# Other durations in the in-kernel list scheduler of a two-layer transformer block

## The chip, the cores and the metric

The kernel runs on one core of one Trainium2 chip. The metric is device time in microseconds (us) of one execution. TensorE (PE) multiplies, VectorE (DVE), ScalarE (ACT) and GpSimd (POOL) do the element work, and SyncE (SP) issues the DMAs. Each engine takes its instructions in the order in which they were written to it and waits on semaphores for what it reads, so a late input holds everything behind it on that engine.

## What is computed

Two layers on an input of 2 x 512 x 512, all in float32. `_layernorm`, attention and feed-forward are the usual ones:

```python
x = L0_attn_hidden_states                                        # (2, 512, 512)
x = x + _layernorm(_L0_attn_ref(_layernorm(x), Wq, Wk, Wv, Wo))  # 32 heads, 8 for K and V, rotary, causal
x = x + _layernorm(_L0_ffn_ref(_layernorm(x), A, B, W, bias))    # one linear map with a low-rank part
x = x + _layernorm(_L1_attn_ref(_layernorm(x), Wq, bq, ...))     # 32 heads, q and k normalised, not causal
x = x + _layernorm(_L1_ffn_ref(_layernorm(x), w1, w3, w2, ...))  # silu(h1) * h3, width 1376, low-rank parts
```

## The kernel before

**Tiling.** Tokens are tiles of 128 rows (four per batch), features are chunks of 128, and head size is 128. A product is made exact to float32 from halves: every operand is split into hi + lo in a faster 32-bit matmul format, and `mm3` (line 393) adds hi hi, hi lo and lo hi in PSUM. So each operand costs a copy (hi) and a subtraction (lo) on the other engines, and TensorE runs three matmuls in place of one.

**Work.** A unit is two heads of one batch: 32 units for layer 0, 32 for layer 1, then six feed-forward units for each batch. A unit has projections, scores with softmax, the product of P^T with V, and the output projection that is added to `y`. In most units ("lag") P^T is not made on TensorE: `softmax_tail` (line 681) transposes 32 x 32 blocks on VectorE, stores them to a DRAM buffer (`pc` in layer 0, `pd` in layer 1), reads them back with the blocks in place, and makes hi (a copy on ACT or DVE) and lo (a subtraction on POOL or DVE). In layer 1, q and k take a similar way (`flip`, line 1097, through `kdq` and `kdk`). Only then can `av_items` (line 839) issue the matmuls into `ps_oy` that use P^T.

**What sets the order.** The order of all instructions is computed while the program is built, by a list scheduler in the kernel's own code. It keeps a clock in us for each engine:

- `Engine.cost` (line 70) gives the duration of an ACT, DVE or POOL instruction from its engine, its operation, the number of columns and whether its source is PSUM.
- `Engine.__getattr__` (line 98) issues the instruction and advances the engine's clock. For a DMA it sets when the transfer is expected to have landed. For the others it keeps in `banks` when a PSUM bank is next usable, and in `last` when the result can be read.
- `mm`, `tp` and `pe` (lines 388, 401, 378) advance TensorE's clock.
- A piece of work is a generator. When it yields nothing, its next stage is put off until `last`, the time at which its newest result is expected (`step`, line 273).
- `streams` (line 345) walks a main list (scores, then P^T V) and streams of fills (`q` and `v` projections, `o` output projections, `a` the P^T V of lagged heads). It issues the next main item if what it reads is expected to be there and its tiles are free, and else a fill, from up to `ahead` places further on.
- `pick` (line 127) chooses, for a subtraction, addition, scaling or copy, the engine with the least expected end plus its duration times a weight; the weights and `ahead` differ by phase (`PHASES`). In the long phase of layer 1 they are 0.5 for DVE and 0.25 for POOL and ACT.

These clocks never enter the program. They only decide the order on each engine's queue and the choices of `pick`; semaphores do the waiting on the chip. PSUM has eight banks in the planner's list, and the large SBUF tiles are slots of one arena, named `ar` in the profile; all instructions stand at line 102, where `Engine.__getattr__` issues them.

Of the kernel before, what the change touches and what calls it, by code (L numbers as in the profile page):

```python
# [21 lines left out]
P = 128  # L22
# [7 lines left out]

LAT = 0.1
FIRST = "x0 x1 x2 k x3 q r v y o z"
# [24 lines left out]
class Item:  # L57
    """a piece of TensorE's work, to be issued when cond holds"""

# [4 lines left out]
class Engine:  # L64
    """An engine that keeps its order of issue, with a clock (us) of its work."""

# [3 lines left out]
    def cost(self, op, args, kw):  # L70
        out = args[0]
        n = 1
        for d in out.shape[1:]:
            n *= d
        src = args[1] if len(args) > 1 else out
        if op in ("bn_stats", "tensor_reduce"):
            n = max(n, nbytes(src) // (4 * src.shape[0]))
        psum = getattr(src, "space", None) == PSUM
        if self.name == "scalar":
            c = n / 1200 + (0.05 if psum else 0.093)  # L80
            for x in ("scale", "bias", "accum_out"):
                c += 0.093 if isinstance(kw.get(x), bass.AP) else 0
            return c
        if op in ("bn_stats", "bn_aggr"):
            return n / 960 + 0.2
        if self.name == "vector" and op == "tensor_scalar" and not psum:
            return n / 1326 + 0.07
        if self.name == "vector":
            return n / 960 + 0.07
        if op == "memset":  # L90
            return n / 960 + 0.07
        if len(args) > 3 and args[3] == ALU.pow:
            return 0.169 * n + 0.27
        if op == "tensor_tensor":
            return 0.00217 * n + 0.115
        return 0.00083 * n + 0.245

    def __getattr__(self, op):
        f = getattr(self.eng, op)

        def g(*args, **kw):
            r = self.k.tc.keep_in_program_order(f(*args, **kw))  # L102
            if self.name == "sync":
                k = self.k
                ram = args[0].space == bass.MemoryType.DRAM
                run = 4 * args[0].shape[-1]
                k.hw = max(k.hw + (0.62 if ram else 0.475), k.now + 0.6)
                k.dma = max(k.dma, k.hw + 0.6) + nbytes(args[0]) / 0.36e6 * (2 if run < 512 else 1)
                k.last = max(k.last, k.dma + 0.9)
            elif self.name in ("scalar", "vector", "gpsimd"):  # L110
                k = self.k
                t = max(self.free, k.now + LAT)
                banks = {x.name for x in args if isinstance(x, bass.AP) and x.space == PSUM}
                for x in banks:
                    t = max(t, k.banks.get(x, 0.0))
                self.free = t + self.cost(op, args, kw)
                for x in banks:
                    k.banks[x] = self.free + LAT
                k.last = max(k.last, self.free)
            return r  # L120
# [3 lines left out]
class Engines:  # L124
    WEIGHT = dict(vector=1.0, scalar=0.5, gpsimd=0.0)

    def pick(self, *cands):
        """issue the one of the candidates (engine, op, args...) that is done first"""
        def score(x):
# [20 lines left out]
    def mul(self, out, a, s):  # L150
        """by a factor of each row"""
        self.pick(("gpsimd", "tensor_scalar", out, a, s, 1.0, ALU.mult, ALU.mult),
# [3 lines left out]
    def copy(self, out, a):  # L156
        """from PSUM"""
        self.pick(("scalar", "copy", out, a), ("vector", "tensor_copy", out, a))
# [8 lines left out]
class Kern:  # L167
    """Work is written as items: functions, or generators that yield the time
    (of TensorE's work) after which their next stage is to be issued."""

# [30 lines left out]

# [1 line left out]
    def slot(self, tag):  # L203
# [12 lines left out]

    # the large tiles: a half or the whole of a slot each (halves of one type only in a slot)
    HALF = dict(W=2, Wk=1, nat=2, v=2, PT=2, TN=2, KT=2, raw=1, bb=1, bqk=1, qk=1, P=1, x=1, A=1, T=1, xn=1, pt=1, ot=1,
# [52 lines left out]

# [1 line left out]
    def step(self, g):  # L273
# [22 lines left out]
    def phase(self, i):  # L296
        """what is tuned for each phase of the work"""
        for k, v in PHASES[i].items():
# [26 lines left out]
    def wait(self, tag, n=1):  # L325
        """in a stage: until n slots are free, first come first served"""
        q = self.queues.setdefault(tag, [])
# [6 lines left out]
    def low(self, eng):  # L334
        """in a stage of low priority: until the engine has nothing issued to it"""
        e = getattr(self.nc, eng)
# [8 lines left out]
    def streams(self, main, fills, bg):  # L345
        """Issue the streams of items, each in its order: a fill when its nominal place in
        main has come, or main waits; bg starts at its nominal place."""
        mi = bi = idle = 0
# [27 lines left out]

# [1 line left out]
    def pe(self, t):  # L378
        """t: at the full clock, which TensorE has after a busy tick only"""
        s = max(self.clk, self.now)  # L380
# [7 lines left out]
    def mm(self, out, l, r, start, stop):  # L388
        self.nc.tensor.matmul(out, l, r, start=start, stop=stop)
        n = r.shape[-1]  # L390
        self.pe(n / 2400 + 0.0026 if r.dtype == F32R else n / 600 + 0.005)

    def mm3(self, out, pairs, start=True, stop=True):
        """exact hi/lo products: hi hi + hi lo + lo hi"""
        n = len(pairs)
# [5 lines left out]
    def tp(self, out, in_):  # L401
        self.nc.tensor.transpose(out, in_, self.ident)
        self.pe(0.109)

# [1 line left out]
    def setup(self):  # L406
# [33 lines left out]

# [1 line left out]
    def split(self, hi, lo, raw):  # L442
        """hi + lo = raw exactly"""
        nc = self.nc
# [33 lines left out]

# [1 line left out]
    def ln_stats(self, src):  # L480
# [68 lines left out]
    def resid(self, b, tt, lvl):  # L549
        """x of level lvl + 1 = x + LN(y); returned short of a constant of each row"""  # L550
        nc = self.nc
# [42 lines left out]
    def boundary(self, b, tt, lvl):  # L594
        """from the finished y of level lvl on"""
        x = yield from self.resid(b, tt, lvl)
# [18 lines left out]

# [1 line left out]
    def out_proj(self, b, first, last, ot, w, badd, lvl):  # L617
        """y += O Wo over the heads of this unit"""
        def one(tt):
# [61 lines left out]
    def softmax_tail(self, st, j, qt, ps, bias, scale, w):  # L681
# [13 lines left out]
        if not st.get("lag"):  # L695
            st["p", j, qt] = pr
            return
        # P^T = 32 x 32 blocks transposed on VectorE, and the blocks put in place on their way through DRAM
        yield from self.wait("T")
# [60 lines left out]
    def unit_done(self, st):  # L760
        """after the last use of V"""
        if st["vlast"]:
# [4 lines left out]
    def pv_items(self, st, j, voff, causal, bias):  # L767
        """transposes of P, then O^T = V^T P^T, split"""
        box = {}
# [69 lines left out]
    def av_items(self, st, j, voff, bias):  # L839
        """O^T = V^T P^T by halves of the queries, split"""  # L840
        box = {}
# [41 lines left out]

# [1 line left out]
    def l0_init(self):  # L885
# [11 lines left out]
    def l0_zero(self):  # L897
        """the parts of pd0 that stay unused"""
        nc = self.nc
# [113 lines left out]

# [1 line left out]
    def l1_init(self):  # L1015
# [18 lines left out]
    def l1_pre(self, hp, b, w, lag):  # L1034
# [62 lines left out]
        def flip(n):  # L1097
            """the transposes as 32 x 32 blocks on VectorE, put in place on their way through DRAM"""
            nat = st["nat" + n]
# [92 lines left out]

# [1 line left out]
    def f0_init(self):  # L1194
# [38 lines left out]

# [1 line left out]
    def f1_init(self):  # L1235
        """rows 0:16, 32:48, 64:80 of the pieces: hi of a low-rank factor, lo in block k; others 0"""
        nc, a = self.nc, self.a
# [150 lines left out]
    def f1_post(self, js, b, sts, last):  # L1388
        """y += g W2 over the chunks of units js"""
        def one(tt):  # L1390
# [29 lines left out]

# [1 line left out]
    def run(self, nu0=16, nu1=16, nf=6):  # L1422
        # at the ends of a layer's units some run batch by batch, each then with weights of its own
        units = []
# [17 lines left out]
        def pre(n):  # L1442
            """early, mid items and state of unit n"""
            if n not in sts:
# [43 lines left out]
        for k in FIRST.split():  # L1488
            for f in todo[k]:
                self.do(f)  # L1490
        # weights start this many units before (early, mid, late parts)
        bgs = {}
# [143 lines left out]
def _layout(i):  # L1636
    """Layouts of the arrays only: transposes and tilings."""
    n = {k: np.asarray(v) for k, v in i.items()}
# [44 lines left out]
```

## Time and profile before

| | |
|---|---|
| time, median of 3 runs | 2113.08 us (2110.2 to 2115.16) |
| span of the profiled execution | 2117.8 us |
| mean granted TensorE clock | 0.993 |
| TensorE, VectorE, ScalarE, GpSimd busy | 97%, 85%, 63%, 68% of the span |
| TensorE matmuls; VectorE instructions | 12605; 4210 |
| DMA | 370.54 MB, 175 GB/s in the mean |

The profile comes from one execution, for which it gives the span from the first to the last instruction. The names are tiles of the program: `ps_pj` projections, `ps_s` scores, `ps_oy` P^T V and output products, `ps_tr` transposes, `ar` any large tile. In a list of groups, a line has engine, operation, output and inputs, shape and count, then the busy us in total and the mean ns of one, then the engine's idle time before these and what ended it. A list of waits has the waiting instruction, who ended the wait, the us in total, how many times, and the longest. A releaser is inferred from semaphores.

### The profile page before, as it was taken

Reading aid. Unit: us, or ns where it says so; the run is one execution under the profiler, and the core shown is the slowest. Engines: PE = TensorE matmul, PEld = TensorE weight load, DVE = VectorE, ACT = ScalarE, POOL = GpSimd, SP = SyncE. Lnnn points to the kernel's source line nnn. Section 1 sums busy time; section 2 is a strip of 40 time slices with the busy share of each in tenths; the row PEclk is TensorE's granted clock in tenths of the full one; section 3 lists DMA queues with packets and bytes.
Section 4 is the critical chain, followed back from the end, with each engine's and each line's share of the span. In section 5 each row is a group of like instructions: output and inputs, shape, how many; then the busy total and the mean of one; then the engine's idle time right before and its main releaser. Section 6 shows DMA issues by size and latency. Waiting matters only on the chain.

```text
span 2117.8 us, 41211 instructions
## 1 busy us (share of the span) xinstructions
PE 2056.7 (97%) x12605; PEld 1827.5 (86%) x12605; DVE 1801.4 (85%) x4210; ACT 1337.7 (63%) x3247; POOL 1446.3 (68%) x1786
## 2 busy tenths in 40 slices
PE   8999999999999999999999999999999999989998
PEld 7888888888888798889899999999999898977886
DVE  7998899899888889889889999899989988888534
ACT  5776677577766668776666666666667666664212
POOL 5686678688875567877677777777777776774212
PEclk9999999999999999999999999999999999999999
DMA  2476567577652235887877777777777787763021
GB/s 98 127 183 166 145 185 183 143 200 199 177 159 66 71 103 166 244 232 223 227 202 229 220 227 211 207 221 219 225 206 232 213 240 212 224 178 93 31 67 44
DMA packets 476566, 370.54 MB, mean 175 GB/s; under 512 B 117400, under 2 KB 424488, under 8 KB 476344
## 3 DMA queue, kind: packets, MB, share of 16 engines
q1 hardware_dynamic: 476344, 367.91, 60.9%
q8 instruction: 99, 1.62, 0.3%
q14 instruction: 123, 1.01, 0.2%
HBM read 232.12 MB, written 135.66 MB: 174 GB/s over the span
## 4 chain that ended last, share of the span: by engine, by line
PE 54%; DMA 12%; DVE 9%; SPq 3%; issue 2%; POOL 2%; ACT 2%; DVEq 0%; ACTq 0%; POOLq 0%
PE ps_pj L102 23%; PE ps_oy L102 19%; PE ps_s L102 10%; DVE ar L102 6%; SPq L102 3%; DMA pd<-ar 3%; DMA ar<-pd 2%; POOL ar L102 2%; DMA kdk<-ar 2%; ACT ar L102 2%; DMA ar<-kdq 2%; DMA kdq<-ar 2%; PE ps_tr L102 1%; DMA ar<-pc 1%; DVE m L102 1%
## 5 line engine op out<-in xcount | busy, mean ns | idle before, releaser
L102 POOL TENSOR_TENSOR ar<-ar,ar 128x256 fp32r<-128x256 f32 (+4 forms) x1223 | 1058.3, 887 | 456.6 <-ACT ar L102 333.6
L102 PE MATMUL ps_oy<-ar,ar 128*128 128x256 f32 (+2 forms) x4014 | 832.2, 342 | 28.7 <-DVE ar L102 14.0
L102 PEld LDWEIGHTS ps_oy<-ar,ar 128*128 128x128 f32 x4014 | 653.5, 190 | 133.1 <-DVE ar L102 22.5
L102 ACT CAST ar<-ar 128x256 fp32r<-128x256 f32 (+3 forms) x1166 | 531.5, 490 | 305.4 <-DMA ar<-pd 117.1
L102 PE MATMUL ps_pj<-ar,xh 128*128 128x256 f32 (+1 forms) x3392 | 635.2, 285 | 0.9 <-POOL ar L102 0.6
L102 PEld LDWEIGHTS ps_pj<-ar,xh 128*128 128x128 f32 x3392 | 536.0, 190 | 14.5 <-POOL ar L102 1.1
L102 PE MATMUL ps_pj<-ar,xl 128*128 128x256 f32 (+1 forms) x1696 | 482.9, 285 | 0.0
L102 DVE STREAM_TRANSPOSE ar<-ar 128x256 f32<-128x256 f32 (+3 forms) x688 | 347.9, 533 | 16.9 <-DMA pd<-ar 9.7
L102 DVE TENSOR_TENSOR ar<-ps_pj,ar 128x512 f32<-128x512 f32 (+2 forms) x448 | 305.4, 683 | 52.5 <-PE ps_pj L102 44.8
L102 PE MATMUL ps_s<-ar,ar 128*128 128x512 f32 (+2 forms) x1252 | 338.5, 376 | 8.6 <-DVE ar L102 4.7
L102 PEld LDWEIGHTS ps_pj<-ar,xl 128*128 128x128 f32 x1696 | 322.9, 190 | 2.1 <-DVE xl L102 0.7
L102 PE MATMUL ps_pj<-xh,ar 128*128 128x512 f32 x816 | 286.6, 399 | 0.7 <-ACT xh L102 0.7
L102 DVE TENSOR_TENSOR y<-ps_oy,y 128x512 f32<-128x512 f32 x272 | 184.8, 680 | 81.8 <-PE ps_oy L102 80.2
L102 PEld LDWEIGHTS ps_s<-ar,ar 128*128 128x128 f32 x1252 | 214.5, 189 | 44.0 <-DVE ar L102 12.6
L102 DVE TENSOR_TENSOR ar<-ar,ar 128x256 fp32r<-128x256 f32 (+5 forms) x328 | 207.9, 652 | 51.1 <-ACT ar L102 50.1
L102 ACT ACTIVATE ar<-ps_s,mr,rq 128x512 f32<-128x512 f32 x256 | 198.6, 777 | 46.7 <-DVE mr L102 36.9
L102 PEld LDWEIGHTS ps_pj<-xh,ar 128*128 128x128 f32 x816 | 154.0, 189 | 31.7 <-ACT xh L102 1.1
L102 DVE TENSOR_REDUCE m<-ps_s 128x1 f32<-128x512 f32 x256 | 170.9, 673 | 6.2 <-PE ps_s L102 5.0
L102 ACT ACTIVATE ar<-ar,ri 128x512 f32<-128x512 f32 (+3 forms) x245 | 149.6, 621 | 38.3 <-DVE ri L102 37.1
L102 POOL TENSOR_SCALAR ar<-ar,ri 128x512 f32<-128x512 f32 (+3 forms) x202 | 133.0, 661 | 54.3 <-DVE ri L102 48.9
L102 PE MATMUL ps_pj<-xl,ar 128*128 128x512 f32 (+1 forms) x408 | 161.2, 395 | 0.0
L102 ACT ACTIVATE ar<-ps_s,m 128x512 f32<-128x512 f32 (+3 forms) x256 | 133.8, 526 | 23.4 <-DVE m L102 14.8
(91 smaller groups left out, 2105.5 us busy)
## 6 DMA issues: line engine op xcount, KB each, us to landing
pd<-ar SPq DMA_DIRECT2D x240, 256.0 KB, 3.7
ar<-pd SPq DMA_DIRECT2D x480, 128.0 KB, 3.3
ar<-pc SPq DMA_DIRECT2D x200, 128.0 KB, 3.0
ar<-in_wq SPq DMA_DIRECT2D x86, 256.0 KB, 4.1
ar<-in_wo SPq DMA_DIRECT2D x86, 256.0 KB, 3.6
kdk<-ar SPq DMA_DIRECT2D x31, 512.0 KB, 4.8
ar<-kdk SPq DMA_DIRECT2D x124, 128.0 KB, 4.0
kdq<-ar SPq DMA_DIRECT2D x31, 512.0 KB, 5.1
```

Of the source, the lines that this page charges most:

```text
L102: r = self.k.tc.keep_in_program_order(f(*args, **kw))
```

## The change

Only the scheduler's figures change; `PHASES` and all loops stay. Matmuls become longer (`COL` us per column and 0.006 each, at least 0.109). A matmul now also marks its PSUM bank as readable only `PTAIL + LAT` after its end. The time between two dependent instructions, a flat 0.1, becomes 0.06 plus a `TAIL` of the engine that wrote. The landing of a DMA is expected 1.0 us later. Several DVE, ACT and POOL durations change: DVE instructions with an SBUF source get longer, an accumulated sum on ACT costs 0.2, the power function on POOL gets a larger fixed part. Comments and documentation strings that the diff also removes are left out here.

```diff
-LAT = 0.1
+LAT = 0.06
+TAIL = dict(scalar=0.1, vector=0.078, gpsimd=0.04)
+PTAIL = 0.175
+LAND = 1.9
+COL = 0.0004395
...
         if self.name == "scalar":
-            c = n / 1200 + (0.05 if psum else 0.093)
-            for x in ("scale", "bias", "accum_out"):
-                c += 0.093 if isinstance(kw.get(x), bass.AP) else 0
+            c = n / 1200 + (0.06 if psum else 0.095) + (0.2 if "accum_out" in kw else 0)
+            for x in ("scale", "bias"):
+                c += 0.095 if isinstance(kw.get(x), bass.AP) else 0
             return c
         if op in ("bn_stats", "bn_aggr"):
-            return n / 960 + 0.2
+            return n / 960 + 0.15
         if self.name == "vector" and op == "tensor_scalar" and not psum:
-            return n / 1326 + 0.07
+            return max(n / 870, 0.07)
         if self.name == "vector":
-            return n / 960 + 0.07
+            return n / 960 + (0.07 if psum else 0.12 if n > 8 else 0.07)
         if op == "memset":
             return n / 960 + 0.07
         if len(args) > 3 and args[3] == ALU.pow:
-            return 0.169 * n + 0.27
+            return 0.16 * n + 0.4
         if op == "tensor_tensor":
-            return 0.00217 * n + 0.115
+            return 0.00217 * n + 0.14
         return 0.00083 * n + 0.245
...
-                k.last = max(k.last, k.dma + 0.9)
+                k.last = max(k.last, k.dma + LAND)
...
                 self.free = t + self.cost(op, args, kw)
+                done = self.free + TAIL[self.name]
                 for x in banks:
-                    k.banks[x] = self.free + LAT
-                k.last = max(k.last, self.free)
+                    k.banks[x] = done + LAT
+                k.last = max(k.last, done)
...
     def mm(self, out, l, r, start, stop):
         self.nc.tensor.matmul(out, l, r, start=start, stop=stop)
         n = r.shape[-1]
-        self.pe(n / 2400 + 0.0026 if r.dtype == F32R else n / 600 + 0.005)
+        self.pe(max(n * COL + 0.006, 0.109) if r.dtype == F32R else 4 * n * COL)
+        self.banks[out.name] = self.clk + PTAIL + LAT
...
     def tp(self, out, in_):
         self.nc.tensor.transpose(out, in_, self.ident)
         self.pe(0.109)
+        self.banks[out.name] = self.clk + PTAIL + LAT
```

## The prediction

> **What bounds the kernel now.** First the page's shares of busy time, then the slices: matmul runs nearly everywhere, VectorE (DVE) is next.
>
> ```profile
> PE 2056.7 (97%) x12605; PEld 1827.5 (86%) x12605; DVE 1801.4 (85%) x4210; ACT 1337.7 (63%) x3247; POOL 1446.3 (68%) x1786
> ```
>
> A busy share of 97% does not tell how much of it is waiting, because a matmul counts as busy from its start to its drained end. So next the timeline of TensorE in a dense stretch, where the start of one matmul to the start of the next is its real price.
>
> ```profile
> 1605.21 0.40 PE L102 MATMUL ps_pj<-ar,xh 128*128 128x256 f32 x2
> 1605.45 0.28 PE L102 MATMUL ps_pj<-ar,xl 128*128 128x256 f32 x1
> 1605.57 0.40 PE L102 MATMUL ps_pj<-ar,xh 128*128 128x256 f32 x2
> 1605.81 0.28 PE L102 MATMUL ps_pj<-ar,xl 128*128 128x256 f32 x1
> ```
>
> Three matmuls of 256 columns take 0.36 us, 0.12 each, though each shows 0.28 busy. Over the whole trace the median step from start to start is 119 ns (256 columns, 7156 of them), 231 (512, 4445), 175 (384, 384), 109 (348 transposes, and each of 256 records of the full-precision products). The sum, with 3.4 us for eight large full-precision records, is 851.6 + 1026.8 + 67.2 + 37.9 + 27.9 + 3.4 = 2014.8 us. The first matmul starts at 7.3 us, the last at 2107.8: 2100.5 us of stream, so 85.7 us of steps longer than their median, and 17.3 us at the two ends. That is all the order of issue can touch: 4% of the span.
>
> Where it is lost shows in the count of matmuls per stretch of 53 us (columns: stretch, its length, then busy us and count of PE, PEld, DVE, ACT, POOL, granted clock, DMA share, GB/s).
>
> ```profile
> 848.00:901.00 53.00, 50.57 (x347) 45.83 (x347) 47.38 (x106) 39.07 (x91) 43.85 (x53) 1.00 0.86 247
> 901.00:954.00 53.00, 49.25 (x318) 44.33 (x318) 44.44 (x93) 39.41 (x88) 41.15 (x50) 0.97 0.80 232
> 1590.00:1643.00 53.00, 53.00 (x384) 49.93 (x383) 49.13 (x114) 35.78 (x82) 39.27 (x46) 1.00 0.79 232
> 1749.00:1802.00 53.00, 49.48 (x316) 45.12 (x315) 42.92 (x95) 33.48 (x78) 35.30 (x41) 0.94 0.75 205
> 1855.00:1908.00 53.00, 45.09 (x240) 37.19 (x239) 47.33 (x104) 36.20 (x74) 37.59 (x52) 0.94 0.59 165
> ```
>
> With the same mix of work, 384 matmuls fit where nothing waits, and only 318 and 316 in the lead-in and the end of layer 1's attention. By steps, the 85 us fall so: 5.8 us to 53; 8.3 in 53 to 583; 10.8 in 583 to 795 (change of layer); 22.9 in 795 to 1060 (lead-in of layer 1); 9.2 in 1060 to 1696; 12.4 in 1696 to 1855; 14.1 in 1855 to 1908 (change to the last feed-forward); 1.5 after. The granted clock of 0.94 is a consequence of the stops, inside the sum.
>
> Last the waits: whom TensorE waits for, then who stops the queues behind it (engine and what it issues, who ended the wait; us in total, times, longest).
>
> ```profile
> PE ps_oy L102 <- DVE ar L102: 14.0, 17, 2.2
> PE ps_tr L102 <- ACT ar L102: 11.4, 7, 7.3
> PE ps_oy L102 <- POOL ar L102: 8.5, 14, 1.5
> ```
> ```profile
> ACT ar L102 <- PE ps_pj L102: 161.0, 87, 8.8
> ACT ar L102 <- DMA ar<-pd: 117.1, 62, 4.2
> ACT ar L102 <- PE ps_oy L102: 70.2, 76, 5.2
> ```
> ```profile
> SPq L102 <- DMA pd<-ar: 212.8, 105, 4.7
> ```
>
> TensorE waits for halves of P^T that DVE or POOL has not finished; upstream ScalarE (ACT), in order, sits on landings and PSUM groups that have not come, with later work behind it, and SP's queue holds its next DMAs behind stores not yet landed.
>
> **The change part by part.** No instruction is added or removed by a duration. What moves is the order on each queue, and through `pick` which engine takes a subtraction, copy or scaling.
>
> *Matmuls.* The old plan charges 7156 x 0.1093 + 4445 x 0.2159 + 384 x 0.1626 + 37.9 + 128 x 0.2183 + 3.4 = 1873 us (two records are one full-precision product). The new charges 0.1185, 0.2310, 0.1748 and 0.225: 2012 us, the trace's 2015. The old plan's TensorE thus ran 7% ahead. One rule speaks against the change: the Trainium skill's page "TensorE: Matmul & The Clock Gate", section "Back-to-back issue gap", gives an isolated step as columns / 2.4 + 2.5 ns, 215.8 and 109.2 ns, just the old charges; it adds that weight loads move the spacing in a real stream. By the rule the new charge is 7% too high and 1873 us of work would leave 227 us of stalls; by the row (119 and 231 ns, with next to no waits in 1590 to 1643) there are 86. I take the row.
>
> *Landings (LAND 0.9 to 1.9).* From the planner's formula a 128 KB read from `pd` lands 0.475 + 0.6 + 0.36 + 0.9 = 2.34 us after its issue begins, now 3.34; a 256 KB store 2.85, now 3.85.
>
> ```profile
> pd<-ar SPq DMA_DIRECT2D x240, 256.0 KB, 3.7
> ar<-pd SPq DMA_DIRECT2D x480, 128.0 KB, 3.3
> ```
>
> The rows say 3.7 and 3.3: the new figure is right to 0.2. Each P^T goes through both, so the old plan is 2.0 us early there.
>
> *Visibility (LAT, TAIL, PTAIL).* One hop was 0.1; it becomes 0.16 behind ACT, 0.138 behind DVE, 0.10 behind POOL and 0.235 behind a matmul. A PSUM addition of 512 was 0.603 and stays so, plus the 0.078 tail = 0.681; its row has 680 ns.
>
> *Vector instructions.* A 512 exponential with its sum was 0.756, now 0.877. A 256 subtraction on DVE goes from 0.337 to 0.387, on POOL from 0.670 to 0.696.
>
> ```profile
> L102 DVE TENSOR_TENSOR ar<-ar,ar 128x256 fp32r<-128x256 f32 x223 | 134.3, 621 | 23.5 <-ACT ar L102 23.0
> L102 POOL TENSOR_TENSOR ar<-ar,ar 128x256 fp32r<-128x256 f32 x853 | 641.5, 769 | 300.8 <-ACT ar L102 236.3 <-DVE ar L102 36.7 <-DVE r L102 11.3
> ```
>
> With tail and LAT the DVE subtraction is now expected after 0.525 (before 0.437), against 0.621 busy: still early, by less. In the long phase of layer 1 the weights are 1.5 on DVE and 1.25 on POOL and ACT: a subtraction's scores move 44 ns towards POOL, a copy 75 ns towards ACT, a 512 scaling from DVE 0.684 against ACT 0.766 to 0.883 against 0.771. So scalings leave DVE: 53 of 320 are there, 53 x 0.669 = 35 us at most over the kernel, spread on ACT (63% busy) and POOL (68%). Of the 223 subtractions perhaps 30 move, 30 x 0.77 = 23 us of POOL. Both are hidden: POOL is busy 39 to 44 of 53 us in the rows above. Without that cover each late subtraction would be a wait of TensorE of 0.15 us (0.769 less 0.621), 4.5 us.
>
> *What it is worth.* A P^T chain is expected 2.0 (landings) + 0.12 (exponential) + 0.14 (scores visible) + about 0.25 (subtraction, hops) = 2.5 us later than before. Most of the stops are single steps under 2.4 us, within the plan's error, so an order made with the right figures can put other matmuls there. Lower bound of the effect in 795 to 1060 and 1696 to 1855: nothing; upper bound: all 35.3. I take half, 17.6, since there is other work (projections) but PSUM has only eight banks. In the two changes of layer (24.9) the chain is layernorm, transposes and weights, with no detour through DRAM: I take a fifth, 5. Ends (17.3): unchanged, since nothing else exists to be put there. Places that ran well and are reordered by chance: 8 lost, bounded by 0 and by the slower rival. Net 17.6 + 5 - 8 = 14.6, so 2117.8 - 15 = 2103 us of span. The page gives the profiled execution by its span alone; that stands 4.7 us above the runs' median of 2113.1, and I carry this over: 2098.
>
> Nobody is made to wait by a new semaphore. What is late next, where a stop goes, is DVE: 47 to 49 of 53 us busy.
>
> **The rivals.** *A, the repair above*, 2098. For it: ACT idles 117 us on `pd` landings and 231 on matmul groups, SP 213 on stores, all waits that a late expectation reorders. Against it: in 1060 to 1696 the same errors of the plan cost only 9 us. Own range: 2078 (all 35 us regained) to 2108 (5 regained).
>
> *B, nothing to gain.* The chains are really too long for the lead-in, and the steady stages keep their slack: 2109 to 2117, I say 2113. For it: nearly no stall in 636 us of layer 1 despite a 7% error.
>
> *C, fills overtake the chain; slower.* With P^T expected 2.5 us later, the stream lets projections and output products go first (up to `ahead`, 15 to 45 places). Their PSUM additions, 0.68 us each, enter DVE's queue ahead of the transpose or subtraction that P^T needs, and DVE has only 4 to 6 us free in 53. Place: layer 1's attention from 795 to 1855, 30 of its units of two heads. It decides where the additional DVE work before a subtraction exceeds the chain's slack. At one more late addition for each of 60 heads it is 60 x 0.68 = 41 us, less A's 15: 2113 + 26 = 2139; with two, 2180. For it: the steady part, 1060 to 1696, can only lose. Against it: matmuls charged 7% more give DVE more room in the plan, and scalings leave it.
>
> **How the numbers follow.** A 0.52, B 0.10, C 0.38. The time is A's, 2098. About 0.2%, 4 us, is what the measurement can tell from no change: faster takes 0.50 (A without its upper edge), same 0.12, slower 0.38. The range starts at A's low end less a little, 2080, and reaches into C past its first price to 2150; 1 in 10 lies above (two late additions), under 1 in 10 below. A's own range is 2078 to 2108.
>
> **What would show it.** Right: over 345 matmuls in the stretches at 901 and 1749; ACT's wait for `pd` well under 117 us and SP's for `pd` stores under 213; ACT's waits for `ps_pj` and `ps_oy` under 231; fewer DVE scalings than 53; the same medians of 119 and 231 ns. Wrong: more long steps in 1060 to 1696 than 9 us, with `ps_oy` waiting for DVE, which is C; or those waits of ACT and SP gone while TensorE's long steps stay near 85 us, which is B: then they were never on its path. A new stop at a change of layer above 14 us would also break the forecast.

## The result, and the profile after

The change is a little slower: 2118.8 us in the median of 9 runs (2117.5 to 2131.0) against 2111.5 of before in the same comparison (2104.2 to 2115.3), a ratio of 1.0055, interval 1.0035 to 1.0076. The forecast was 2098, faster. The range held the time; the direction was wrong.

First a warning that the two profiles give. The span after is 2115.8 us, which is less than the 2117.8 of the profile before. The execution profiled after took 2117.64 us as a run, so a run is its span plus 1.8 us. By that the execution profiled before took 2119.6 us, longer than any of its timed runs: it was an unusually long one. A second profile of the same kernel (e1 below) has a span of 2109.0. It is the one to compare with.

The page's shares, of the profile after:

```profile
PE 2049.8 (97%) x12605; PEld 1824.6 (86%) x12605; DVE 1762.6 (83%) x4125; ACT 1358.4 (64%) x3285; POOL 1477.3 (70%) x1831
```

There are as many matmuls as before; VectorE has 85 instructions fewer, POOL 45 and ACT 38 more. `pick` has moved work, as the new durations make it. The median steps from start to start of a matmul are again 119, 231, 175 and 109 ns, so it is once more only the long steps that differ.

The counts of matmuls per stretch of 53 us, after (stretch, length, busy us and count of PE, PEld, DVE, ACT, POOL, clock, DMA share, GB/s):

```profile
689.00:742.00 53.00, 46.11 (x260) 37.92 (x259) 45.83 (x123) 33.63 (x79) 28.86 (x46) 1.00 0.24 80
901.00:954.00 53.00, 49.38 (x344) 45.30 (x343) 47.73 (x98) 40.22 (x95) 42.67 (x47) 1.00 0.89 257
1590.00:1643.00 53.00, 52.49 (x383) 49.47 (x382) 45.97 (x106) 34.90 (x80) 41.23 (x51) 1.00 0.80 231
1749.00:1802.00 53.00, 50.00 (x341) 45.43 (x340) 45.89 (x96) 37.02 (x83) 43.43 (x51) 1.00 0.84 226
1855.00:1908.00 53.00, 44.64 (x235) 36.48 (x234) 47.63 (x103) 34.25 (x69) 31.68 (x46) 0.94 0.51 149
```

and of before in its second profile:

```profile
689.00:742.00 53.00, 50.42 (x293) 42.03 (x293) 44.86 (x116) 32.05 (x74) 25.96 (x48) 1.00 0.22 75
901.00:954.00 53.00, 50.34 (x331) 45.73 (x330) 44.65 (x94) 38.28 (x86) 41.48 (x49) 0.97 0.79 236
1749.00:1802.00 53.00, 49.20 (x322) 45.12 (x321) 42.12 (x97) 33.53 (x78) 36.04 (x46) 0.94 0.81 223
```

The end of layer 1's attention is better (322 to 341), its lead-in a little (331 to 344). The new loss is in 689 to 742, at the change from layer 0 to layer 1: 293 matmuls became 260, and TensorE's busy time fell by 4.3 us.

Who stops which queue, after: ACT first, then SP's queue, then TensorE.

```profile
ACT ar L106 <- PE ps_pj L106: 172.6, 90, 8.5
ACT ar L106 <- PE ps_oy L106: 105.6, 103, 6.1
ACT ar L106 <- DMA ar<-pd: 67.8, 44, 4.8
```
```profile
SPq L106 <- DVE ar L106: 387.8, 218, 29.4
SPq L106 <- DMA pd<-ar: 152.7, 83, 4.7
```
```profile
PE ps_oy L106 <- POOL ar L106: 13.4, 19, 2.5
PE ps_oy L106 <- DVE ar L106: 12.1, 14, 2.4
PE ps_tr L106 <- ACT ar L106: 11.3, 2, 7.7
```

The waits on landings fell as the new landing figure says they should: ACT for `pd` from 117.1 to 67.8 us (108.4 in the second profile of before), SP for `pd` stores from 212.8 to 152.7 (211.2). TensorE gained nothing from it. It still waits for the same halves of P^T, now longer for POOL (8.5 to 13.4), and SP waits longer for VectorE's blocks (275.4 to 387.8).

To place the long steps, the stages are bounded here by the count of matmuls started, not by time, so that all kernels can be laid side by side. In us beyond the median step of a matmul of as many columns (231 ns for all of 512, in every kernel); times of the stages are those of the second profile of before:

| stage | before, 2nd profile | after |
|---|---|---|
| start, to 105 | 6.1 | 5.4 |
| layer 0, 105 to 588 | 6.6 | 10.7 |
| change of layer, 588 to 775 | 10.6 | 13.5 |
| lead-in of layer 1, 775 to 1022 | 20.0 | 21.6 |
| steady layer 1, 1022 to 1699 | 8.3 | 7.3 |
| its end, 1699 to 1863 | 14.3 | 9.7 |
| last feed-forward | 12.0 | 15.1 |
| all | 77.8 | 83.3 |

The difference of 5.5 us, and 1.2 us more before the first and after the last matmul, make that of the spans (6.8). The first profile of before has 86.6 us by this measure; the prediction's 85 us price eight full-precision records at their own 428 ns.

### The profile page after: what moved, and what is told of

Its sections match the earlier page's. It is cut to its first block, busy times and chain, and to the rows that moved or that the text cites. A ratio compares the mean times of both kernels' runs of the same rounds, so it can differ in the third digit from the quotient of the medians.

```text
span 2115.8 us, 41243 instructions
## 1 busy us (share of the span) xinstructions
PE 2049.8 (97%) x12605; PEld 1824.6 (86%) x12605; DVE 1762.6 (83%) x4125; ACT 1358.4 (64%) x3285; POOL 1477.3 (70%) x1831
## 5 line engine op out<-in xcount | busy, mean ns | idle before, releaser
L106 POOL TENSOR_TENSOR ar<-ar,ar 128x256 fp32r<-128x256 f32 (+3 forms) x1268 | 1093.4, 886 | 404.2 <-ACT ar L106 299.7
L106 PE MATMUL ps_oy<-ar,ar 128*128 128x512 f32 (+2 forms) x4014 | 829.1, 341 | 29.2 <-POOL ar L106 13.4
L106 PEld LDWEIGHTS ps_oy<-ar,ar 128*128 128x128 f32 x4014 | 652.9, 189 | 134.2 <-POOL ar L106 20.4
L106 ACT CAST ar<-ar 128x256 fp32r<-128x256 f32 (+3 forms) x1190 | 543.2, 489 | 227.2 <-DMA ar<-pd 67.8
L106 PEld LDWEIGHTS ps_s<-ar,ar 128*128 128x128 f32 x1284 | 220.9, 189 | 39.1 <-POOL ar L106 7.1
L106 DVE TENSOR_TENSOR ar<-ar,ar 128x256 fp32r<-128x256 f32 (+6 forms) x290 | 197.1, 691 | 39.1 <-ACT ar L106 37.0
L106 POOL TENSOR_SCALAR ar<-ar,ri 128x512 f32<-128x512 f32 (+3 forms) x228 | 149.6, 659 | 82.9 <-DVE ri L106 63.2
```

## The experiments

Three theories stood at first: (1) fills overtake the P^T chain, rival C of the prediction; (2) the new instruction costs move work to POOL, and that is the loss; (3) the loss is that of any new order. A fourth came out of the first four runs.

**e1: before again.**

> The kernel before, unchanged, as a yardstick. Every theory expects a ratio of 1.000 within 0.002. Its profile tells whether the 85 us of long TensorE steps in the first profile are typical: the span of that profile (2117.8 us) is longer than its timed runs (2104 to 2115), so I expect some 75 us of long steps and a span near 2109 here.

Measured: 1.0006 (0.9995 to 1.0017), span 2109.0, 77.8 us of long steps. As expected; the first profile was 8.8 us longer.

**e2, e3, e4: one part of the change each** (the lines of the change that use the new names of e4 are left out here).

```diff
e2  -        self.pe(n / 2400 + 0.0026 if r.dtype == F32R else n / 600 + 0.005)
    +        self.pe(max(n * COL + 0.006, 0.109) if r.dtype == F32R else 4 * n * COL)
e3  -                k.last = max(k.last, k.dma + 0.9)
    +                k.last = max(k.last, k.dma + 1.9)
e4  -LAT = 0.1
    +LAT = 0.06
    +TAIL = dict(scalar=0.1, vector=0.078, gpsimd=0.04)
    +PTAIL = 0.175
```

> Only the matmul durations (COL) are changed. Theory 1 (fills overtake the P^T chain, because landings and results are expected later): no loss, 0.995 to 1.000. Theory 2 (the new instruction costs move subtractions and scalings to GpSimd): 1.000. Theory 3 (the order of before is a lucky draw, and any new order costs about the same): 1.004 to 1.008.

> Only the expected landing of a DMA is 1.0 us later. Theory 1: this is most of the loss, 1.004 to 1.010, with more long steps before ps_oy in 1060 to 1696. Theory 2: 1.000. Theory 3: 1.004 to 1.008, as for any other new order. By all of them the waits of ScalarE for pd landings fall well under 117 us.

> Only LAT, TAIL and PTAIL are changed: results are expected 0 to 0.14 us later. Theory 1: a small part of the loss, 1.001 to 1.004. Theory 2: 1.000. Theory 3: 1.004 to 1.008.

Measured: e2 1.0426 (1.0402 to 1.0450), e3 1.0042 (1.0026 to 1.0058), e4 1.0093 (1.0072 to 1.0113). No theory had the first, and e4 too lies above all of them (1.008 at most). The one figure that the trace supports best, the step of a matmul, costs 90 us when it is put in alone. In e2, three stretches of the steady part of layer 1, and TensorE's waits from 1060 to 1696:

```profile
1219.00:1272.00 53.00, 51.46 (x358) 47.31 (x357) 47.92 (x108) 34.10 (x78) 39.49 (x45) 1.00 0.72 213
1272.00:1325.00 53.00, 49.25 (x332) 45.24 (x331) 41.94 (x95) 32.52 (x76) 33.40 (x42) 0.97 0.67 199
1378.00:1431.00 53.00, 51.61 (x345) 47.21 (x344) 42.76 (x97) 31.20 (x73) 34.51 (x41) 0.97 0.63 187
```
```profile
PE ps_s L103 <- DVE ar L103: 12.0, 9, 1.8
PE ps_s L103 <- ACT ar L103: 3.1, 4, 1.4
PE ps_oy L103 <- POOL ar L103: 1.6, 1, 1.6
```

The second and third of these stretches in the second profile of before:

```profile
1272.00:1325.00 53.00, 52.49 (x382) 49.19 (x381) 47.91 (x111) 34.43 (x80) 39.33 (x50) 1.00 0.76 227
1378.00:1431.00 53.00, 51.91 (x368) 47.93 (x367) 48.47 (x109) 34.27 (x79) 39.77 (x46) 1.00 0.75 228
```

The steady stage loses there: 332 matmuls for 382 and 345 for 368, its long steps are 33.6 us (before 8.3), and the clock of 0.97 shows a spell of half clock in each. VectorE and POOL are less busy than before in those stretches, so the loss does not look like more work on them: TensorE stands before inputs that are not ready. In e3 the opposite: the steady stage has 2.8 us, which speaks against theory 1, and its end 4.8 (before 14.3), but the change of layer 23.3 (before 10.6).

From this came theory 4: **two errors of the old plan cancel.** A chain through DRAM is two landings (3.6 and 3.4 us for `pd` in the trace after) and the work of three engines around them; what the order needs to know is how many matmuls go by meanwhile. Matmuls too short by 7% make it look longer, landings too early make it look shorter. I thought of the chain of P^T, but in the steady stage of e2 the trace shows another: of its 33.6 us, 25.1 stand before score matmuls (`ps_s`), which read the halves of q and k, and only 2.1 before the products of P^T with V. q and k go through DRAM as well. The P^T products follow the last score of their head by 133 to 178 matmuls in e2's steady stage, and by as many in e3's. By which step of the plan the scores come too early was not followed further.

**e5: matmuls and landings together (e2 and e3).**

> Matmul durations and landings changed together, visibility and instruction costs as before. Theory 4, new (two errors of the old plan cancel: matmuls too short make a P^T chain last more matmuls in the plan, landings too early make it last fewer; taking away the first alone let the plan issue matmuls right behind inputs that are not there): the later landing gives back more than half of the loss of matmuls alone, 1.005 to 1.020. Theory 3 (any new order costs alike, parts don't interact): 1.047, the sum of 1.0426 and 1.0042, or anything.

Measured: 1.0083 (1.0068 to 1.0099). The later landing takes back four fifths of e2's loss: the steady stage falls from 33.6 to 14.0 us, the lead-in from 39.8 to 20.2. The parts do not add (their sum is 1.047), which theory 4 said. Two of the stretches shown for e2, here:

```profile
1272.00:1325.00 53.00, 52.37 (x370) 48.69 (x369) 45.51 (x106) 32.53 (x78) 37.20 (x47) 1.00 0.70 206
1378.00:1431.00 53.00, 53.00 (x378) 49.71 (x377) 47.42 (x107) 34.99 (x81) 39.43 (x50) 1.00 0.71 218
```

**e6, e7: the change less one part.** Against the changed kernel; all of `cost` goes back in e6:

```diff
e6  -            return max(n / 870, 0.07)
    +            return n / 1326 + 0.07
...
e7  -        self.pe(max(n * COL + 0.006, 0.109) if r.dtype == F32R else 4 * n * COL)
    +        self.pe(n / 2400 + 0.0026 if r.dtype == F32R else n / 600 + 0.005)
```

> The whole change without the new instruction costs. Theory 2 (the new costs' shift from VectorE to GpSimd is the loss): 0.998 to 1.001. Theory 4: the costs are a small part of the chain's length, some 0.1 us, so it stays within 0.004 of the change's 1.0055, rather above it: 1.005 to 1.010.

> The whole change with the old, short matmul durations. Theory 4: chains look long twice over, so the steady stages keep next to no long steps and the loss sits at the changes of layer: 1.003 to 1.012. If the true matmul durations were what costs the change its time, this would be 0.99 to 1.000.

Measured: e6 1.0053 (1.0038 to 1.0068): without the new instruction costs the loss is the same, which speaks against theory 2 as far as one order can tell. e7 1.0142 (1.0111 to 1.0172), above what I expected, steady stage 3.3 us, layer 0 26.7, change of layer and lead-in 46.4.

But e7 computes a wrong output (relative error 0.054), so its time shows nothing of the true matmul step. The likely reason is in its order. Heads use three DRAM buffers `pc` in turn, and nothing in the kernel holds the store of a head back until the reads of the head three before it are issued. With stores and reads of each half of `pc` counted in order, 16 stores of e7 go out before those reads, the first at 549.3 us; no other kernel here has one. So the planner's clocks decide more than the time: a set of figures can make an order that overwrites data. That a condition on these stores mends the output was not tried.

**e9: matmuls with landings of 2.9**, against e5:

```diff
-                k.last = max(k.last, k.dma + 1.9)
+                k.last = max(k.last, k.dma + 2.9)
```

> New matmul durations with landings expected yet another 1.0 us later (2.9, which the rows of DMA issues do not support). Theory 4 (the plan's margin between chain and matmuls decides the steady stages): long steps of TensorE in the steady two fifths of layer 1 fall from 14 us (matmuls and landings of 1.9) to 8 or less, and the ratio to 1.002 to 1.008. Theory 5 (a truthful figure is best): they rise again, ratio above 1.0083.

Measured: 1.0189 (1.0175 to 1.0203), a miss. The steady stage fell less than I said, from 14.0 to 10.0 us; the change of layer and the lead-in rose from 36.4 to 52.3, layer 0 from 10.0 to 16.0. So margin is not a cure by itself.

**e8, e11, e12: before, with the last digit of one figure changed.**

```diff
e8   -LAT = 0.1
     +LAT = 0.101
e11  -                k.last = max(k.last, k.dma + 0.9)
     +                k.last = max(k.last, k.dma + 0.92)
e12  -        self.pe(n / 2400 + 0.0026 if r.dtype == F32R else n / 600 + 0.005)
     +        self.pe(n / 2400 + 0.0027 if r.dtype == F32R else n / 600 + 0.005)
```

> Before, with LAT 0.101 in place of 0.100: the same model within 1 ns in a hop, yet another order. Theory 3 (the order of before is a lucky draw): 1.003 to 1.008. Theory 4: only what the model says of a chain counts: 0.998 to 1.002.

> Before with a landing of 0.92 in place of 0.90: another order from the same model. Theory 3: 1.002 to 1.008, with the loss at the changes of layer, not in the steady stages. Theory 4 alone: 0.998 to 1.002.

> Before with 0.0027 in place of 0.0026 us added to each matmul: another order from the same model. Theory 3: 1.002 to 1.008, with the loss at the changes of layer. Theory 4 alone: 0.998 to 1.002.

Measured: 1.0029 (1.0008 to 1.0050), 1.0068 (1.0052 to 1.0083), 1.0071 (1.0057 to 1.0085). The same model, another order, and two of three as slow as the change. Theory 3 holds, though not in its detail: the loss is not at the change of layer (9.8 to 10.6 us in all three, before 10.6) but in the last feed-forward (17.2, 17.6, 23.7 against 12.0) and, for e8 and e11, in the steady stage (11.7 and 14.5 against 8.3).

**e13, e14, e15: the change, disturbed as little.**

```diff
e13  -LAT = 0.06
     +LAT = 0.061
e14  -LAND = 1.9
     +LAND = 1.92
e15  -        self.pe(max(n * COL + 0.006, 0.109) if r.dtype == F32R else 4 * n * COL)
     +        self.pe(max(n * COL + 0.0061, 0.109) if r.dtype == F32R else 4 * n * COL)
```

> The change with LAT 0.061 in place of 0.060. Scatter alone (both models alike, before a favourable draw): 1.002 to 1.010, around the change's 1.0055. If the new figures cost time by themselves: all of e13 to e15 at 1.005 or above. If the change was an unlucky draw of a better model: most below 1.003.

> The change with LAND 1.92 in place of 1.90. As for e13: scatter 1.002 to 1.010; a cost of the figures, 1.005 or above in all three; an unlucky draw, below 1.003 in most.

> The change with 0.0061 in place of 0.0060 us for each matmul. As for e13: scatter 1.002 to 1.010; a cost of the figures, 1.005 or above in all three; an unlucky draw, below 1.003 in most.

Measured: 1.0097 (1.0067 to 1.0126), 1.0067 (1.0052 to 1.0082), 1.0026 (1.0015 to 1.0036). The four orders of the changed model lie at 1.0061 in the mean, the four of the old model at 1.0042, and at 1.0056 without the one that was there. By stages, as means of four and the lowest and highest of them:

| stage | old figures | new figures |
|---|---|---|
| layer 0 | 8.0 (6.6 to 9.3) | 8.5 (4.7 to 10.7) |
| change of layer | 10.3 (9.8 to 10.6) | 16.3 (13.5 to 18.6) |
| lead-in of layer 1 | 18.0 (15.6 to 20.4) | 22.9 (21.2 to 25.4) |
| steady layer 1 | 9.9 (5.3 to 14.5) | 5.9 (4.0 to 8.4) |
| its end | 14.0 (13.6 to 14.3) | 9.8 (8.0 to 11.0) |
| last feed-forward | 17.6 (12.0 to 23.7) | 17.6 (15.1 to 19.8) |
| all, with the start | 83.8 (77.8 to 88.3) | 87.3 (78.8 to 96.7) |

Here the change can be read with less of the luck of one order. It gains at the end of layer 1's attention and loses at the change of layer and in the lead-in, and in those rows the two sets do not overlap. In the steady stage it gains in the mean, with overlap. At the change of layer the four are hardly four draws, though: there the old orders have the same kind of matmul (outputs, inputs, shape) at 95 to 99% of TensorE's places, and three of the new ones at 91 to 96%, with e14 apart. So that row compares one old order with two new ones, and a good order that small disturbances keep would look the same as a loss by the figures.

**e10, e16: new figures from the fifth unit of layer 1 on, the order of before up to there** (the expectations count units from 0 and say fourth). e10 takes over the landing alone, e16 all figures of the change, with the same switch in each formula.

`phase(i)` is called with i = 3 there.

```diff
e10  +        self.land = 1.9 if i >= 3 else 0.9
     -                k.last = max(k.last, k.dma + 0.9)
     +                k.last = max(k.last, k.dma + k.land)
```

> Before, with the later landing (1.9) only from the fourth unit of layer 1 on; up to there the order is that of before. Landing alone lost 17 us of long steps around the change of layer and saved 17 in layer 1 and its end. If places are independent (theory 4: margin helps where chains go through DRAM in a steady stream), the saving stays without the loss: 0.992 to 0.997. Theory 3 (luck of order): anywhere from 0.997 to 1.006.

> The old figures up to the third unit of layer 1, all of the change's from the fourth on. If the changed model helps where chains go through DRAM in a steady stream, as the later landing alone did: 0.993 to 0.998. If only the landing in that setting helps, since true matmul durations take the margin away again: 0.998 to 1.006.

Measured: e10 0.9942 (0.9930 to 0.9954), 2095.6 us; e16 0.9968 (0.9958 to 0.9979). Both are faster than both kernels. In e10:

```profile
1696.00:1749.00 53.00, 52.55 (x363) 48.65 (x363) 47.43 (x104) 37.95 (x90) 39.11 (x48) 1.00 0.77 229
1749.00:1802.00 53.00, 50.22 (x354) 46.08 (x353) 48.12 (x110) 37.46 (x85) 35.99 (x40) 1.00 0.86 249
```

In the second stretch 354 matmuls against 322 of before; the end of layer 1's attention has 5.7 us of long steps (before 14.3), the steady stage 3.8 (8.3).

**e17, e18: e10, disturbed** (against e10; in e18 `self.lat` also takes the place of `LAT` where it is used).

```diff
e17  -        self.land = 1.9 if i >= 3 else 0.9
     +        self.land = 1.92 if i >= 3 else 0.9
e18  +        self.lat = 0.101 if i >= 3 else 0.1
```

> e10 with a landing of 1.92 in place of 1.90 from the fourth unit of layer 1 on; everything before it in the order of before. If the later landing is worth its 17 us of long steps in layer 1 whatever the order: 0.991 to 0.998. If e10 was luck: up to 1.004.

> e10 with LAT 0.101 in place of 0.100 from the fourth unit of layer 1 on. As for e17: the margin's gain 0.991 to 0.998, luck up to 1.004.

Measured: e17 0.9951 (0.9934 to 0.9969), e18 1.0013 (0.9998 to 1.0028), a miss: its steady stage has 14.7 us and the end 10.4. Three orders of this model lie at 0.9969 in the mean. The gain is likely the later landing's, since the end of the attention is below the old model's four in each of the three (5.7, 3.6, 10.4 against 13.6 to 14.3). It is so in all 13 orders here with a later landing (3.6 to 12.3 us); the six without it have 11.1 to 20.1. But the size of the gain in any one kernel is luck.

## Why the prediction was wrong

**The term that failed is "half, 17.6"**, for the lead-in and the end of layer 1's attention. In the changed kernel they gave 3.0 us (end 4.6 gained, lead-in 1.6 lost), in the means of four orders -0.7 (4.2 gained, 4.9 lost). Behind the term stood the step that the waits of ACT and SP for landings lie on TensorE's path, so that an order which ends them gives TensorE its time back. These waits fell as forecast (ACT on `pd` 117 to 68, SP on `pd` stores 213 to 153; VectorE's scalings of 512 went from 53 to 22), and TensorE's long steps rose from 77.8 to 83.3. That is close to the sign set for rival B: the waits were, in the main, not on TensorE's path. e3 shows it more sharply: ACT's wait for `pd` is down to 25.8 us, and the long steps are 85.2. The end of the attention is the exception. The two stretches that were to pass 345 matmuls came close, with 344 and 341.

ACT's waits for matmul groups, which were to fall below 231, rose to 278 (172.6 + 105.6): ACT waits 49 us less for `pd` and 47 us more for matmuls. The time moved from one wait to another.

**"A fifth, 5"** failed too. I had TensorE regain 5 us in the two changes of layer. In the means the first of them lost 6.0 us (10.3 to 16.3), and the last feed-forward, which holds the second, did not move; in the changed kernel they lost 2.9 and 3.1. With 4.0 gained in the steady stage, where I expected nothing, the stages sum to +3.5 us of long steps, 83.8 to 87.3: a model no better than the old one.

**The price of TensorE's work** was right: 119 and 231 ns again. I took the row against the isolated step of the Trainium skill's page "TensorE: Matmul & The Clock Gate" (section "Back-to-back issue gap"), which gives 109.2 and 215.8 ns, the old charges. But that these should make the worse plan did not follow: e2 shows them as the better ones beside the old landings.

**"Places that ran well and are reordered by chance: 8 lost"** was the right mechanism, and its size was about right. Three new orders of the old model cost 0.29, 0.68 and 0.71%, 6 to 15 us, before any figure is better or worse. This alone is enough for the change's 0.55%; the difference between the means of the two models, 0.19%, is within their scatter. I had it as one term of a sum; beside the other terms as measured it was the largest.

**The step from span to time** was also wrong: I carried over 4.7 us by which one profile stood above the median, and that was the length of one execution, not a relation (a run is its span plus 1.8). The range held the time only because it reached into rival C's prices.

**Rival C** ended on the right side for another reason. Its sign was more long steps in the steady part, and that did not lose: 7.3 us against 8.3. That it is not C's mechanism there is shown by e3, where later landings bring that stage to 2.8.

**Open.** Why the change of layer suffers is not settled, nor whether any order unlike the old one would suffer there. Every part alone raises it (matmuls to 16.2 us, landings 23.3, visibility 19.0, before 10.6), and in the changed kernel its costliest step, 2.8 us before a `ps_pj` product of 512 columns, waits for ACT; which item the plan should have put there was not tried. Whether the new figures with other `PHASES` would beat the old ones was not tried either.

## What to carry to other kernels

A planner's figures work as a set: replace one by its true value and errors that cancelled show, so measure the parts alone and together, and look at the stage where the margin acts. Before reading anything into a fraction of a per cent from a reordered schedule, disturb both versions in a digit that cannot matter and see how far they scatter. Take a second profile of the baseline when its span doesn't lie where its timed runs do. And let conditions, not expected times, keep a buffer from being overwritten, since every figure changes the order.

## What the runs showed of the hardware

Two profiles of one kernel had 86.6 and 77.8 us of long TensorE steps in the same order of issue, 8.8 us of span apart, with 6 and 5 spells of half clock among the matmuls (23.9 and 27.3 us). Each of these spells, and each in e2 and in the changed kernel, follows stops of TensorE of 1.7 us or more in the 7 us before it. A stop can so cost more than its length: inside the spells of e2 the median step of 512 columns is 427 ns, not 231. In e2 there are 14 such spells, 58.0 us in all. Their matmuls lose some 22 us against their medians, 10 in the second profile of before: about 12 of the 78 us that e2's long steps have more.
